# Two sigmoids in place of one in a GRU step, and another order of the first loads

## The chip, the cores and the metric

One core of one Trainium2 chip runs the kernel, as one program. The time is device microseconds (us) of that core for one execution. Smaller is better. The kernel before takes 594.6 us, the median of seven runs from 593.49 to 597.3 us.

## The reference

The input x has 2 sequences of 1024 steps of 256 numbers, all in float32. The first layer adds to x what a two-layer GRU makes of it, and the second adds to that a mixture of experts (a shared one, and two of eight experts for each token). Of the GRU, all that matters here is one step. Its gates r (reset), z (update) and n (new) are made of a product of the step's input and a product of the state before it:

```python
h0 = zeros; mixed = tanh(x @ W_in.T + b_in + context)
xg = mixed @ Wih.T + bih                 # all steps at once
def step(h, xt):                         # 1024 times, one after the other
    hg = h @ Whh.T + bhh
    r = sigmoid(xr + hr)
    z = sigmoid(xz + hz)
    n = tanh(xn + r * hn)
    return (1 - z) * n + z * h
```

The second layer of the GRU runs the same step over the states of the first.

## The kernel before

**The stages.** The kernel loads its weights, runs both GRU layers, and then the mixture of experts (`moe`). The change lies in the GRU and in the loads ahead of it. At the very end stands a second, slow GRU behind `tc.If`, for inputs on which the first one isn't exact; it isn't taken here.

**The GRU in ticks.** Each sequence of 1024 steps is cut into J = 16 chunks of S = 64 steps that run side by side, and each chunk warms its state up on the steps ahead of it (`AHEAD`: 64 steps for layer 0, 44 for layer 1). So the loop has 64 + 64 + 2 = 130 ticks. Layer 0 runs in ticks 0 to 127, layer 1 in ticks 22 to 129, two steps behind. That makes 128 + 108 = 236 steps of a layer. Two batches times 16 chunks are 32 rows (R); the 256 hidden units lie in four quarters (Q) of 64, each on 32 partitions, so that a gate of all rows is a tile of 128 partitions by 64.

**One step of a layer.** `add_state` (L247) adds the state's product to a PSUM bank in which the input's product already stands. `finish_scanned` then makes the new state:

- L287, ScalarE: one sigmoid over the sums of r and z, 128 by 128, into `gates`. The weights and biases of z were negated at the start, so that this gives 1 - z at once.
- L290, VectorE: a scan, s = r * hn + xn, in the PSUM bank.
- L300, ScalarE: n = tanh, negated.
- L302, VectorE: the part of the state that is kept.
- L305, VectorE: a scan that gives the new state's rows.
- L313, VectorE: the transpose to `h`, which the next tick's L247 needs.

ScalarE also copies the next step's starting sums into a bank (`prepare`, L421): of layer 0 from `inputs`, of layer 1 the bias `bt`. In ticks with both layers, TensorE adds the input's product of layer 1 (`feed`, L219).

**Order.** `tc.manual_schedule` fixes the order of the loop as the code has it. On each engine the instructions run in that order, and wait for each other by semaphores.

**Inputs of layer 0.** `inputs` holds the starting sums of 64 steps. A `mix` piece (L196 products, L208 tanh) makes `mixed` of 256 columns of x (MB); an input piece (L219 products, L366 the bias) makes one step's inputs of it. Two mix pieces and four input pieces stand ahead of the loop; the ticks take the rest, two to a tick while layer 0 runs alone, else one. L354 writes the first quarter of every step's `inputs` (a bias) in one VectorE copy.

**The loads.** SP's queue issues, in this order: `w_in`, the first 512 columns of x (two loads), `wih0`, `whh0`, `wih1`, `whh1`, the rest of x, and the weights of `moe`. ScalarE's queue issues `vec`, and eight loads that spread the biases over the partitions (`both`, L126). L165 to L169 add the biases up (`bt`).

Of the kernel before, what the change touches and what calls it, by code (L numbers as in the profile page):

```python
# [8 lines left out]
FP = mybir.dt.float32  # L9
# [3 lines left out]
AF = mybir.ActivationFunctionType  # L13
ALU = mybir.AluOpType
# [3 lines left out]
P = 128  # L18
# [3 lines left out]
KD = D // P  # L22
N = B * T
# [3 lines left out]
Q = 4  # L27
U = D // Q
WIDE = 6 * U + 8
R = P // Q  # L30
J = R // B
S = T // J
# [9 lines left out]
TB = 512  # L42
MB = 256
# [20 lines left out]
def gru_moe(ctx, tc, xT, vec, bias, w_in, wih0, whh0, wih1, whh1, w_out, w_gate, router, w1, w3, w2, w1e, w2e, out):  # L64
    nc = tc.nc
    const = ctx.enter_context(tc.tile_pool(name="const", bufs=1))

    def weights(src, k, m, name, pool=const):
        t = pool.tile([P, k, m], FP, name=name)
        nc.sync.dma_start(out=t, in_=src.rearrange("(k p) m -> p k m", p=P))  # L70
        return t
# [5 lines left out]
    def cols(i):  # L77
        return slice(R * i, R * (i + 1))
# [5 lines left out]
    x_sb = const.tile([P, KD, N], FP, name="x_sb")  # L84
    xT_v = xT.rearrange("(k p) n -> p k n", p=P)

    def load_x(n0):
        for k in range(KD):
            nc.sync.dma_start(out=x_sb[:, k, n0 : n0 + TB], in_=xT_v[:, k, n0 : n0 + TB])

    load_x(0)
    hs1 = const.tile([P, KD, N], FP, name="h1")
    count = const.tile([P, 1], I32, name="count")
    ones = const.tile([P, 1], FP, name="ones")
# [15 lines left out]
    class Steps:  # L110


        def __init__(self, stack, tag, on_pe, less_z):
            def pool(name, **kw):
                return stack.enter_context(tc.tile_pool(name=name + tag, **kw))

            self.gru_only = gru_only = pool("gru_only", bufs=1)
            self.edge = edge = pool("edge", bufs=1)
            self.step_pool = pool("step", bufs=3)
            self.p_step, self.p_mix = pool("p_step", bufs=1, space=PSUM), pool("p_mix", bufs=2, space=PSUM)  # L120
            self.sums, self.rows, self.states, self.starts, self.start_rows = ({} for _ in range(5))
            both = []
            for layer in range(2):
                t = edge.tile([P, 2, 3, U], FP, name=f"both{layer}")
                for q in range(Q):
                    nc.scalar.dma_start(  # L126
                        out=t[cols(q)].rearrange("p i g u -> p (i g u)"),
                        in_=bias[layer, q : q + 1, :].to_broadcast([R, 2 * 3 * U]),
                    )
                both.append(t)  # L130
            wih0_sb = weights(wih0, KD, 3 * D, "wih0_sb", gru_only)
            whh0_sb = weights(whh0, KD, 3 * D, "whh0_sb", gru_only)
            wih1_sb = weights(wih1, KD, 3 * D, "wih1_sb", gru_only)
            whh1_sb = weights(whh1, KD, 3 * D, "whh1_sb", gru_only)
            self.wih, self.whh = (wih0_sb, wih1_sb), (whh0_sb, whh1_sb)
            if less_z:

                for t, i, engine in (
                    (wih0_sb, 1, nc.vector),
                    (whh0_sb, 2, nc.vector),  # L140
                    (wih1_sb, 1, nc.gpsimd),
                    (whh1_sb, 2, nc.gpsimd),
                ):
                    part = t.rearrange("p k (q g u) -> p (k q) g u", q=Q, g=3)[:, :, i, :]
                    engine.tensor_scalar(part, part, -1.0, None, ALU.mult)  # L145

            self.picks = gru_only.tile([P, Q, R], BF, name="picks")
            nc.gpsimd.memset(self.picks, 0.0)  # L150
            for q in range(Q):
                nc.gpsimd.memset(self.picks[32 * q : 32 * q + 3, q, :], 1.0)
            upto = gru_only.tile([P, 3], FP, name="upto")
            nc.vector.memset(upto, 0.0)
            for q in range(Q):
                for i in range(3):
                    nc.vector.memset(upto[32 * q : 32 * q + i + 1, i : i + 1], 1.0)
            only = gru_only.tile([P, 3], FP, name="only")
            nc.vector.tensor_copy(only, upto)
            nc.vector.tensor_tensor(only[:, 1:3], upto[:, 1:3], upto[:, 0:2], ALU.subtract)  # L160
            self.parts, self.sum_bias = {}, []
            for layer in range(2):
                bt = gru_only.tile([P, 4, U], FP, name=f"bt{layer}")
                self.sum_bias.append(bt)
                nc.vector.tensor_copy(bt[:, 0, :], both[layer][:, 1, 2, :])  # L165
                nc.vector.tensor_tensor(bt[:, 1:3, :], both[layer][:, 0, 0:2, :], both[layer][:, 1, 0:2, :], ALU.add)
                nc.vector.tensor_copy(bt[:, 3, :], both[layer][:, 0, 2, :])
                if less_z:
                    nc.vector.tensor_scalar(bt[:, 2, :], bt[:, 2, :], -1.0, None, ALU.mult)  # L169
                if layer not in on_pe:  # L170
                    continue
                part = gru_only.tile([P, 4, U], BF, name=f"part{layer}")
                for i in range(3):
                    rounded = edge.tile([P, 4, U], BF, name=f"rounded{layer}{i}")
                    nc.vector.tensor_copy(rounded, bt)
                    if i < 2:
                        rest = edge.tile([P, 4, U], FP, name=f"rest{layer}{i}")
                        nc.vector.tensor_tensor(rest, bt, rounded, ALU.subtract)
                        bt = rest
                    if i == 0:  # L180
                        nc.vector.tensor_scalar(part, rounded, only[:, 0:1], None, ALU.mult)
                    else:
                        nc.vector.scalar_tensor_tensor(part, rounded, only[:, i : i + 1], part, ALU.mult, ALU.add)
                self.parts[layer] = part
            self.mixed_pool = pool("mixed", bufs=2)
# [92 lines left out]
        def finish_scanned(self, layer, to, tick, after_n, between):  # L278

            ps, h = self.sums[layer], self.rows[layer]
            sums = by_sum(ps)

            gates = self.gates[layer][tick % 2]
            nc.scalar.activation(gates[:, :, :, 1], sums[:, 1:3, :], AF.Sigmoid)  # L287

            s = ps[:, 4 : 4 + 6 * U : 3]
            nc.vector.tensor_tensor_scan(  # L290
                s,
                gates[:, 0, :, :].rearrange("p u i -> p (u i)"),
                ps[:, 0 : 6 * U : 3],
                0.0,
                ALU.mult,
                ALU.add,
            )

            n = self.step_pool.tile([P, U, 2], FP, name=f"n{layer}")
            nc.scalar.activation(n[:, :, 0], s[:, 1 : 2 * U : 2], AF.Tanh, scale=-1.0)  # L300
            after_n()
            nc.vector.scalar_tensor_tensor(n[:, :, 1], gates[:, 1, :, 1], 1.0, h, ALU.subtract, ALU.mult)  # L302
            between()
            row = self.step_pool.tile([P, U, 2], FP, name=f"row{layer}")
            nc.vector.tensor_tensor_scan(  # L305
                row.rearrange("p u i -> p (u i)"),
                gates[:, 1, :, :].rearrange("p u i -> p (u i)"),
                n.rearrange("p u i -> p (u i)"),
                0.0,
                ALU.mult,  # L310
                ALU.subtract,
            )
            nc.vector.transpose(to, row[:, :, 1])  # L313
            self.rows[layer], self.states[layer] = row[:, :, 1], to
# [16 lines left out]


    with ExitStack() as stack:
        g = Steps(stack, "", on_pe=(), less_z=True)
        g.gates = [
            [g.gru_only.tile([P, 2, U, 2], FP, name=f"gates{layer}{i}") for i in range(2)] for layer in range(2)
        ]
# [1 line left out]
            for t in pair:  # L339
                nc.gpsimd.memset(t, 0.0)  # L340
        for n0 in range(TB, N, TB):
            load_x(n0)
        load_later()
        edge = g.edge
        h0_pool = stack.enter_context(tc.tile_pool(name="h0", bufs=4))
# [5 lines left out]


        inputs = g.gru_only.tile([P, S, 4, U], FP, name="inputs")
        nc.vector.tensor_copy(inputs[:, :, 0, :], g.sum_bias[0][:, 0, :].unsqueeze(1).to_broadcast([P, S, U]))  # L354

        def input_piece(i):

# [17 lines left out]
        for bank in banks[0] + banks[1]:  # L375
            for q in range(Q):
                nc.tensor.matmul(
                    out=bank[cols(q), 0 : 6 * U],
# [76 lines left out]
        mixing, making = mix_pieces(), input_pieces()  # L455

        def take(pieces, n):
            return [p for _, p in zip(range(n), pieces)]
# [13 lines left out]
                    yield from take(which, 1)  # L472
            yield from making

        for piece in take(mixing, 2) + take(making, 4):
            for part in piece:
                part()
        in_turn = pieces_in_turn()
# [52 lines left out]
    with tc.tile_pool(name="p_gate", bufs=1, space=PSUM) as p_gate:  # L531
        ps = p_gate.tile([P, KD, B], FP, name="ps_gate")
        for m in range(KD):
            for k in range(KD):
                nc.tensor.matmul(
                    out=ps[:, m, :],
# [11 lines left out]
    for k in range(KD):  # L548
        for b in range(B):
            i = COND + k * B + b  # L550
# [7 lines left out]
    n_fit = nc.values_load(count[0:1, 0:1], min_val=0, max_val=P)  # L558
    with tc.If(n_fit < P):
        with ExitStack() as stack:  # L560
            g = Steps(stack, "_turn", on_pe=(0, 1), less_z=False)

            for n0 in range(0, N, TB):
                load_x(n0)
            all_mixed = g.gru_only.tile([P, KD, N], FP, name="all_mixed")
            for n0 in range(0, N, MB):
                mixed, pieces = g.mix(n0)
# [485 lines left out]
```

## Time and profile before

| what | value |
|---|---|
| median of seven runs | 594.6 us |
| the profiled execution | 594.44 us, of which the span of the trace is 592.6 us |
| loads and first pieces, to the first gates of tick 0 | 0 to 19.01 us |
| ticks of layer 0 alone (22) | gates at 19.01, then one tick every 2.8 us |
| ticks of both layers (106) | about 80 to 375 us |
| mixture of experts | the rest |
| busy: TensorE, VectorE, ScalarE, GpSimd | 552.2, 399.8, 253.2, 75.9 us |

In a view of the timeline, each line has the start, the duration, the engine, the line of the kernel, the operation, what it writes and reads with shapes, and in brackets how long the engine had been idle and what ended that. An instruction's duration includes its start and its drain, so that instructions on one engine may overlap by a part of it. A `q` behind an engine's name means its sequencer (a DMA being issued, for instance). Ends of matmuls are modelled.

### The profile page before, as it was taken

What the parts mean: (1) busy time and instruction counts of PE and PEld (TensorE: products, weight loads), DVE (VectorE), ACT (ScalarE), POOL (GpSimd) and SP (SyncE); (2) the same over time, 40 slices, a digit from 0 to 9 for tenths busy, and PEclk for the clock granted to TensorE, in tenths of its full rate; (3) what the DMA queues carried; (4) which work ended last, traced back from release to release, by engine and by line L of the source; (5) the groups of instructions that cost most, each with busy time, mean ns of one, the idle gap of its engine ahead of it and who ended that gap; (6) DMA issues with size and microseconds to landing.
All of it is one profiled execution on the core that took longest, in us unless ns stands there. A gap on an engine that the chain in (4) does not pass through costs nothing. (4 is left out here: it accounts for less than half of the span.)

```text
span 592.6 us, 18629 instructions
## 1 busy us (share of the span) xinstructions
PE 552.2 (93%) x7508; PEld 349.5 (59%) x7508; DVE 399.8 (67%) x1300; ACT 253.2 (43%) x849; POOL 75.9 (13%) x115
## 2 busy tenths in 40 slices
PE   4999999999999899999999999589999999999995
PEld 2555566667655444544545455347448888874584
DVE  3556678888988788888888888743884333324485
ACT  1333356666656566656666666301223333331100
POOL 1200000000000000000000000100037760007750
PEclk9999999999999999999999999879999999999999
DMA  8950000000000000000000000002114563113351
GB/s 280 363 187 2 1 3 4 4 2 2 4 2 3 2 3 2 2 3 3 3 2 3 3 3 3 1 19 89 36 32 141 167 152 82 63 64 90 111 167 66
DMA packets 22845, 32.12 MB, mean 54 GB/s; under 512 B 3200, under 2 KB 17920, under 8 KB 22752
## 3 DMA queue, kind: packets, MB, share of 16 engines
q1 hardware_dynamic: 18816, 21.12, 10.5%
q0 software_dynamic: 3408, 9.31, 6.2%
q8 instruction: 63, 1.03, 0.7%
q10 hardware_dynamic: 528, 0.40, 0.3%
q14 instruction: 30, 0.25, 0.1%
HBM read 21.52 MB, written 9.31 MB: 52 GB/s over the span
## 5 line engine op out<-in xcount | busy, mean ns | idle before, releaser
L247 PE MATMUL ps_step<-whh_sb,h 128*32 128x192 f32 x3712 | 197.5, 330 | 2.8 <-DVE h L313 2.8
L247 PEld LDWEIGHTS ps_step<-whh_sb,h 128*32 128x32 f32 x3712 | 97.5, 109 | 77.1 <-DVE h L313 60.2
L219 PE MATMUL ps_step<-wih_sb,h 128*32 128x192 f32 x1728 | 127.0, 331 | 11.0 <-ACT ps_step L421 2.5
L305 DVE TENSOR_TENSOR_SCAN row<-gates,n 128x128 f32<-128x128 f32 x236 | 100.2, 425 | 38.5 <-ACT n L300 38.5
L290 DVE TENSOR_TENSOR_SCAN ps_step<-gates,ps_step 128x128 f32<-128x128 f32 x236 | 98.5, 417 | 25.1 <-ACT gates L287 25.1
L300 ACT ACTIVATE n<-ps_step 128x64 f32<-128x64 f32 x236 | 55.0, 233 | 118.8 <-DVE ps_step L290 118.8
L219 PEld LDWEIGHTS ps_step<-wih_sb,h 128*32 128x32 f32 x1728 | 58.9, 109 | 58.8 <-ACT ps_step L421 45.8
L287 ACT ACTIVATE gates<-ps_step 128x128 f32<-128x128 f32 x236 | 68.7, 291 | 39.0 <-PE ps_step L247 35.7
L219 PE MATMUL ps_in<-wih_sb,mixed 128*32 128x192 f32 x1024 | 59.8, 334 | 6.0 <-DVE wih_sb L145 3.4
L313 DVE STREAM_TRANSPOSE h<-row 128x64 f32<-128x64 f32 x236 | 58.0, 246 | 8.1
L902 DVE COPY hT<-ps_hT 128x256 f32<-128x256 f32 x39 | 16.6, 425 | 54.4 <-PE ps_hT L900 54.4
L421 ACT COPY ps_step<-inputs 128x256 f32<-128x256 f32 x128 | 49.7, 388 | 4.9 <-DVE inputs L366 4.9
L219 PEld LDWEIGHTS ps_in<-wih_sb,mixed 128*32 128x32 f32 x1024 | 35.6, 112 | 23.2 <-ACT ps_step L421 6.7
L302 DVE SCALAR_TENSOR_TENSOR n<-gates,row 128x64 f32<-128x64 f32 x232 | 48.4, 209 | 0.0
L640 POOL IOTA lane_i<- 128x128 int32 x1 | 0.2, 240 | 363.9 <-DVE row L305 363.9
L937 POOL DMA_INDIRECT xg<-given,pick x39 | 37.2, 953 | 65.6 <-DVE more L891 54.0
L421 ACT COPY ps_step<-bt 128x256 f32<-128x256 f32 x108 | 40.7, 377 | 3.4
L908 PE MATMUL ps_y<-w2e_sb,hT 128*128 x156 | 40.2, 380 | 1.0 <-DVE hT L902 1.0
L908 PE MATMUL ps_h<-w1e_sb,xT 128*128 x156 | 40.2, 380 | 0.7 <-DVE xT L902 0.7
L978 POOL DMA_INDIRECT yb<-back,slots x32 | 30.7, 960 | 56.3 <-DMA back<-y 46.8
L908 PEld LDWEIGHTS ps_y<-w2e_sb,hT 128*128 128x128 f32 x156 | 29.4, 190 | 5.5 <-DVE hT L902 1.5
L948 ACT ACTIVATE he<-ps_h 128x256 f32<-128x256 f32 x39 | 15.0, 384 | 37.6 <-PE ps_h L908 37.6
(165 smaller groups left out, 492.2 us busy)
## 6 DMA issues: line engine op xcount, KB each, us to landing
back<-y SPq DMA_DIRECT2D x39, 128.0 KB, 1.8
x_sb<-in_xT SPq DMA_DIRECT2D x8, 256.0 KB, 6.1
w1e_sb<-in_w1e SPq DMA_DIRECT2D x1, 2048.0 KB
w2e_sb<-in_w2e SPq DMA_DIRECT2D x1, 2048.0 KB, 18.5
given<-base SPq DMA_DIRECT2D x4, 512.0 KB, 2.8
out_dram<-o SPq DMA_DIRECT2D x16, 128.0 KB, 2.1
wih_sb<-in_wih SPq DMA_DIRECT2D x2, 768.0 KB, 7.7
whh_sb<-in_whh SPq DMA_DIRECT2D x2, 768.0 KB, 7.8
```

The lines of the kernel that those rows point to most:

```text
L219: last = nc.tensor.matmul(out=out[cols(q), :, :], lhsT=given(k), rhs=self.wih[layer][:, k, q * 3 * U : (q + 1) * 3 * U].rearrange("p (g u) ...
L247: nc.tensor.matmul(out=by_sum(self.sums[layer])[cols(q), 0:3, :], lhsT=self.states[layer][:, k, :], rhs=self.whh[layer][:, k, q * 3 * U : ...
L287: nc.scalar.activation(gates[:, :, :, 1], sums[:, 1:3, :], AF.Sigmoid)
L290: nc.vector.tensor_tensor_scan(s, gates[:, 0, :, :].rearrange("p u i -> p (u i)"), ps[:, 0 : 6 * U : 3], 0.0, ALU.mult, ALU.add,)
L300: nc.scalar.activation(n[:, :, 0], s[:, 1 : 2 * U : 2], AF.Tanh, scale=-1.0)
L302: nc.vector.scalar_tensor_tensor(n[:, :, 1], gates[:, 1, :, 1], 1.0, h, ALU.subtract, ALU.mult)
L305: nc.vector.tensor_tensor_scan(row.rearrange("p u i -> p (u i)"), gates[:, 1, :, :].rearrange("p u i -> p (u i)"), n.rearrange("p u i -> p ...
L313: nc.vector.transpose(to, row[:, :, 1])
L421: return nc.scalar.copy(by_sum(banks[layer][tick % 2])[:, 0:4, :], g.sum_bias[1] if layer else inputs[:, position(0, tick) % S, :, :],)
L908: nc.tensor.matmul(out=ps, lhsT=of[:, k, :], rhs=weights_sb[:, bass.ds(e * KD + k, 1), :], start=(k == 0), stop=(k == KD - 1),)
L937: nc.gpsimd.indirect_dma_start(out=xg, out_offset=None, in_=given[:, :], in_offset=bass.IndirectOffsetOnAxis(ap=pick[:, i : i + 1], axis=0),)
L978: nc.gpsimd.indirect_dma_start(out=yb, out_offset=None, in_=back[:, :], in_offset=bass.IndirectOffsetOnAxis(ap=slots[:, c, j : j + 1], axi ...
```

## The change

- The sigmoid of a step becomes two of 128 by 64: one for r, and one of the negated sum of z (scale -1.0), which gives 1 - z. The negations of four weights (L145) and of two biases (L169) go.
- The biases are laid out for all 128 partitions by the host, and come in one load on SP's queue, behind the first x.
- The first load of x has 256 columns in place of 512; the other 256 stand behind `wih0` and `whh0`.
- Each load of x is one DMA for both halves (k).
- The copy L354 covers 8 steps on VectorE, and the other 56 on GpSimd.
- Two input pieces stand ahead of the loop, not four; the ticks take the other two.

```diff
-    def load_x(n0):
-        for k in range(KD):
-            nc.sync.dma_start(out=x_sb[:, k, n0 : n0 + TB], in_=xT_v[:, k, n0 : n0 + TB])
-    load_x(0)
+    def load_x(n0, n):
+        nc.sync.dma_start(out=x_sb[:, :, n0 : n0 + n], in_=xT_v[:, :, n0 : n0 + n])
+    load_x(0, MB)
...
-            both = []
-            for layer in range(2):
-                t = edge.tile([P, 2, 3, U], FP, name=f"both{layer}")
-                for q in range(Q):
-                    nc.scalar.dma_start(
-                        out=t[cols(q)].rearrange("p i g u -> p (i g u)"),
-                        in_=bias[layer, q : q + 1, :].to_broadcast([R, 2 * 3 * U]),
-                    )
-                both.append(t)
+            both = edge.tile([P, 2, 2, 3, U], FP, name="both")
+            nc.sync.dma_start(out=both.rearrange("p l i g u -> p (l i g u)"), in_=bias)
             wih0_sb = weights(wih0, KD, 3 * D, "wih0_sb", gru_only)
             whh0_sb = weights(whh0, KD, 3 * D, "whh0_sb", gru_only)
+            rest_of_x()
             wih1_sb = weights(wih1, KD, 3 * D, "wih1_sb", gru_only)
             whh1_sb = weights(whh1, KD, 3 * D, "whh1_sb", gru_only)
...
-            if less_z:
-                for t, i, engine in (
-                    (wih0_sb, 1, nc.vector),
-                    (whh0_sb, 2, nc.vector),
-                    (wih1_sb, 1, nc.gpsimd),
-                    (whh1_sb, 2, nc.gpsimd),
-                ):
-                    part = t.rearrange("p k (q g u) -> p (k q) g u", q=Q, g=3)[:, :, i, :]
-                    engine.tensor_scalar(part, part, -1.0, None, ALU.mult)
...
-                if less_z:
-                    nc.vector.tensor_scalar(bt[:, 2, :], bt[:, 2, :], -1.0, None, ALU.mult)
...
-            nc.scalar.activation(gates[:, :, :, 1], sums[:, 1:3, :], AF.Sigmoid)
+            nc.scalar.activation(gates[:, 0, :, 1], sums[:, 1, :], AF.Sigmoid)
+            nc.scalar.activation(gates[:, 1, :, 1], sums[:, 2, :], AF.Sigmoid, scale=-1.0)
...
-        g = Steps(stack, "", on_pe=(), less_z=True)
+        g = Steps(stack, "", on_pe=(), rest_of_x=lambda: load_x(MB, TB - MB))
...
-        nc.vector.tensor_copy(inputs[:, :, 0, :], g.sum_bias[0][:, 0, :].unsqueeze(1).to_broadcast([P, S, U]))
+        for engine, i, n in ((nc.vector, 0, MB // R), (nc.gpsimd, MB // R, S - MB // R)):
+            engine.tensor_copy(
+                inputs[:, i : i + n, 0, :], g.sum_bias[0][:, 0, :].unsqueeze(1).to_broadcast([P, n, U])
+            )
...
-        for piece in take(mixing, 2) + take(making, 4):
+        for piece in take(mixing, 2) + take(making, 2):
...
-        "bias": bias,
+        "bias": np.repeat(bias.reshape(Q, -1), R, axis=0),
```

More of the change, by code (lines that the diff above doesn't have):

```diff
@@ L110, in gru_moe, with __init__ @@
     class Steps:
[L113 removed]
+        def __init__(self, stack, tag, on_pe, rest_of_x):
             def pool(name, **kw):
@@ L164, in __init__ @@
                 self.sum_bias.append(bt)
-                nc.vector.tensor_copy(bt[:, 0, :], both[layer][:, 1, 2, :])
-                nc.vector.tensor_tensor(bt[:, 1:3, :], both[layer][:, 0, 0:2, :], both[layer][:, 1, 0:2, :], ALU.add)
-                nc.vector.tensor_copy(bt[:, 3, :], both[layer][:, 0, 2, :])
-                if less_z:
-                    nc.vector.tensor_scalar(bt[:, 2, :], bt[:, 2, :], -1.0, None, ALU.mult)
+                nc.vector.tensor_copy(bt[:, 0, :], both[:, layer, 1, 2, :])
+                nc.vector.tensor_tensor(bt[:, 1:3, :], both[:, layer, 0, 0:2, :], both[:, layer, 1, 0:2, :], ALU.add)
+                nc.vector.tensor_copy(bt[:, 3, :], both[:, layer, 0, 2, :])
                 if layer not in on_pe:
@@ L341, in gru_moe @@
         for n0 in range(TB, N, TB):
-            load_x(n0)
+            load_x(n0, TB)
         load_later()
@@ L560, in gru_moe @@
         with ExitStack() as stack:
-            g = Steps(stack, "_turn", on_pe=(0, 1), less_z=False)
-            for n0 in range(0, N, TB):
-                load_x(n0)
+            g = Steps(stack, "_turn", on_pe=(0, 1), rest_of_x=lambda: load_x(0, N))
             all_mixed = g.gru_only.tile([P, KD, N], FP, name="all_mixed")
@@ L1021 @@
     bias = np.stack(
-        [np.concatenate([quarters(a[f"L0_cond_b{n}{i}"]).reshape(Q, 3 * U) for n in ("ih", "hh")], 1) for i in range(2)]
+        [quarters(a[f"L0_cond_b{n}{i}"]).reshape(Q, 3 * U) for i in range(2) for n in ("ih", "hh")], axis=1
     )
```

## The prediction

> **What bounds the kernel now.** I read the busy times first, then the counts of the costliest groups, then the timeline: of a tick with layer 0 alone, of a tick with both layers, and of the first 20 us. TensorE is busy 93% of the span, but that doesn't make it the bound of the loop; the timeline does.
>
> A tick of layer 0 alone, from one gate sigmoid to the next:
>
> ```profile
> 52.56 0.30 ACT L287 ACTIVATE gates<-ps_step 128x128 f32<-128x128 f32 x1 [0.95 <-PE ps_step L247]
> 52.89 0.43 DVE L290 TENSOR_TENSOR_SCAN ps_step<-gates,ps_step 128x128 f32<-128x128 f32 x1 [0.86 <-ACT gates L287]
> ...
> 53.35 0.23 ACT L300 ACTIVATE n<-ps_step 128x64 f32<-128x64 f32 x1 [0.49 <-DVE ps_step L290]
> 53.47 0.39 ACT L421 COPY ps_step<-inputs 128x256 f32<-128x256 f32 x1
> 53.61 0.42 DVE L305 TENSOR_TENSOR_SCAN row<-gates,n 128x128 f32<-128x128 f32 x1 [0.18 <-ACT n L300]
> ...
> 54.07 0.25 DVE L313 STREAM_TRANSPOSE h<-row 128x64 f32<-128x64 f32 x1
> ...
> 54.37 0.48 PEld L247 LDWEIGHTS ps_step<-whh_sb,h 128*32 128x32 f32 x16 [0.33 <-DVE h L313]
> ...
> 55.36 0.30 ACT L287 ACTIVATE gates<-ps_step 128x128 f32<-128x128 f32 x1 [1.50 <-PE ps_step L247]
> ```
>
> Each starts when the one above it ends (L421 aside): 0.33 + 0.46 + 0.26 + 0.46 + 0.30 + 0.99 = 2.80 us. This is a chain of latencies, and the sigmoid is a link of it. In a tick with both layers:
>
> ```profile
> 355.03 0.43 DVE L290 TENSOR_TENSOR_SCAN ps_step<-gates,ps_step 128x128 f32<-128x128 f32 x1
> ...
> 356.02 0.29 ACT L287 ACTIVATE gates<-ps_step 128x128 f32<-128x128 f32 x1
> 356.22 0.25 DVE L313 STREAM_TRANSPOSE h<-row 128x64 f32<-128x64 f32 x1
> 356.39 0.40 DVE L290 TENSOR_TENSOR_SCAN ps_step<-gates,ps_step 128x128 f32<-128x128 f32 x1
> 356.52 0.48 PEld L247 LDWEIGHTS ps_step<-whh_sb,h 128*32 128x32 f32 x16 [0.33 <-DVE h L313]
> ...
> 357.44 0.29 ACT L287 ACTIVATE gates<-ps_step 128x128 f32<-128x128 f32 x1
> ...
> 357.77 0.43 DVE L290 TENSOR_TENSOR_SCAN ps_step<-gates,ps_step 128x128 f32<-128x128 f32 x1
> ```
>
> Layer 0's scans are 355.03 and 357.77, layer 1's is 356.39. From 355.03 the same chain takes 2.74 us to the next scan of layer 0, so it binds here too, and layer 1 fits in between. VectorE has little room: layer 1's scan starts 0.17 us behind layer 0's transpose, and 0.08 us after its own gates' end (356.31).
>
> The opening:
>
> ```profile
> 6.21 3.75 PE L196 MATMUL ps_mix<-x_sb,w_in_sb 128*128 128x256 f32 x8 [2.85 <-DMA x_sb<-in_xT]
> 10.25 0.20 DVE L165 COPY bt<-both 128x64 f32<-128x64 f32 x1 [6.02 <-DMA both<-in_bias]
> 10.45 1.14 ACT L208 ACTIVATE mixed<-ps_mix,mix_bias 128x128 f32<-128x128 f32 x4 [7.68 <-DVE bt L165]
> 10.67 2.29 DVE L354 COPY inputs<-bt 128x4096 f32<-128x4096 f32 x1
> 12.87 0.42 DVE L145 TENSOR_SCALAR wih_sb<-wih_sb 128x512 f32<-128x512 f32 x1
> 13.39 2.70 PE L219 MATMUL ps_in<-wih_sb,mixed 128*32 128x192 f32 x32 [3.43 <-DVE wih_sb L145]
> 15.21 0.54 DVE L165 COPY bt<-both 128x64 f32<-128x64 f32 x1 [1.49 <-DMA both<-in_bias]
> 16.09 0.61 DVE L366 TENSOR_TENSOR inputs<-ps_in,bt 128x192 f32<-128x192 f32 x2
> 19.01 0.29 ACT L287 ACTIVATE gates<-ps_step 128x128 f32<-128x128 f32 x1 [2.15 <-PE ps_step L247]
> ```
>
> The biases are late twice (10.25 and 15.21), the copy L354 and the negation L145 hold VectorE until TensorE may start at 13.39, and L366 stands behind the second bias. Nothing of this hides anything: the first gates are at 19.01.
>
> **The ticks.** One might expect the scan to start earlier, as it needs r alone, and n's row (128x64, same stride, 0.233 us) prices r's sigmoid below the 0.291 us of the row of both gates. But in the program as built, r's sigmoid raises no semaphore. Its count is added by z's sigmoid, right behind it, and the scan waits for that sum. So both sigmoids are on the chain. Two in a row never occur in the trace before; the nearest row is n followed by a copy that waits for nothing: 53.35 to 53.47, so 0.12 us from start to start. So z starts 0.12 behind r and ends at 0.12 + 0.233 = 0.353 us, against 0.291: 0.062 us more. From below, z could follow r by its elements alone, 0.291 - 0.233 = 0.058, and end at 0.291: nothing more. From above, it could wait for r's end: 0.466, or 0.175 more. I take 0.062, as the row of n and its copy is this engine with this shape in this place.
>
> The Trainium skill ("ScalarE: Activation LUTs", section "What ACT_TABLE_LOAD costs") gives an ACTIVATE a fixed 186 ns and 0.833 ns per element, with an overlap of about 93 ns back to back; its 293 and 239 ns agree with the rows, its overlap is below the row's 0.11 us, and by it the pair would cost 0.092 us more, 12.0 us over 130 ticks.
>
> The path around layer 1 moves alike: its gates reach its scan 0.06 later, from which n, the copy of `bt` and layer 0's next gates follow on ScalarE; between 86 and 89 us that path has no slack either (copy 86.05, gates 86.36), but a tick holds layer 1's delay there once and VectorE's 1.37 us once, so it too gives 2.74 + 0.06. I also see a separate wait for TensorE ahead of each scan on VectorE; the products end before the gates start, so I cost it at nothing. Behind that wait stand L302 and L305 of the layer, for which the next product waits. If it cost VectorE 0.03 us where its scan follows the transpose, the ticks would take 3 us more.
>
> 130 ticks by 0.062 are **8.1 us more**; the bounds are 0 and 22.8 us.
>
> **The opening.** Added up from the rows: `w_in` and the first x are 512 KB as before (`w_in` and the first half of x), so TensorE starts its mixing at about 6.2 again and ends at about 9.7 (3.75 us less a wait of 0.26 for the second half). The biases stand third on the queue, at about 7 to 8; ScalarE has no bias loads to issue, so the tanh of the second piece runs when the products end, to about 10.4. `wih0` was issued at 2.29 and took 7.7 us, so landed at 10.0; before it there were 1.5 MB of SP's loads and part of the 0.4 MB of biases, now 1.7 MB: I keep 10.0. `whh0` landed at 12.3 (6.09 and 6.2), and is now issued some 3 us earlier, past the biases but ahead of the rest of x: 11.5 to 12.3. Two input pieces take 2.70 us cold or 1.70 warm, from 10.4 at the latest: 12.1 to 13.1, L366 and L421 of the first one beside the second. The state's product and the gates take 1.0 us more (18.03 to 19.01): gates at 13.1 to 14.1, so 4.9 to 5.9 us earlier. I take **5.2 us less**.
>
> The rest of x and layer 1's weights are needed later: the former by tick 0's mix piece, behind the product, at 13 to 14 (2.7 MB into the queue; 0.7 us of slack ahead of tick 1's product if it is late), the latter from tick 21 on. The two input pieces that move into the loop stretch its ticks with pieces by two; such a tick takes 86.36 to 89.10 = 2.74 us, the same as one without (357.44 to 360.18), so they cost nothing; uncovered, they would cost TensorE's 0.83 us each. The negations of L145 on GpSimd and VectorE are gone with their 3.9 us, already in the sum.
>
> GpSimd's copy has 56 by 64 = 3584 elements. Nearest rows: the cast of 128 elements at 0.287 and of 8 at 0.188 us give 0.83 ns each, so 3.1 us; L145 on GpSimd, 512 elements in 1.546 us, gives 10.8 us. It starts with the finished biases at about 8.5 and is needed by tick 7's L421. Either is in time, unless it holds up VectorE. The nearest row is L165 at 15.21 under GpSimd's L145 (15.09 to 16.64): 0.54 instead of 0.20 us, held up by 0.34 and not to the end. So I cost it at 0 to 0.3 us. The Trainium skill ("SBUF — State Buffer", its rule of the shared port pair) says that a VectorE copy of this kind or one with two SBUF inputs blocks fully until GpSimd's instruction ends; by that and 3.1 us nothing is lost, as 11.6 is before the first L366.
>
> **Sum.** The profiled execution took 594.44 us (592.6 of span, 1.8 around it), 0.16 below the median. 594.44 + 8.1 - 5.2 = **597.3 us**, slower by 0.5%. About 0.3%, 1.8 us, is what a measurement of this kernel can tell from no change.
>
> **Rivals.**
> 1. Opening and ticks cancel (within 592.8 to 596.4): a tick cost of 0.03 to 0.05, or 6 us and more gained. For it: the terms are close, and 5.2 / 130 = 0.040 us per tick is break-even. Chance 0.24.
> 2. Faster: ScalarE streams z right behind r, so that a tick costs under 0.027 us more and at the least nothing: 594.44 - 5.2 = 589.2. Against it: the 0.12 of n and its copy. In the same direction lies a scan that is released by r alone: 0.058 by 130 = 7.5 less, so 581.7; the waits as built exclude it. Chance 0.08.
> 3. The pair costs 0.09 us or more, or VectorE's extra wait shows: 130 by 0.09 = 11.7, less 5.2, gives 600.9; with no overlap at all 612.0. Chance 0.13.
> 4. GpSimd's copy takes 10.8 us and blocks VectorE: its first L366 waits to about 19.3, the first gates come at about 20.5, and the opening loses 1.5 us: 604.0. Against it: the 0.34 us above. Chance 0.06.
>
> My forecast, 596.4 to 600, has the rest, 0.49. That makes slower 0.49 + 0.13 + 0.06 = 0.68, same 0.24, faster 0.08. The range goes from 594.0 (tick cost 0.042 with 5.9 gained) to 602.0 (0.097 with 5.0 gained), which leaves out some 0.1 at each end.
>
> **What would show it.** Right: the two sigmoids start 0.12 us apart, the scan starts 0.39 us after r (0.33 before), ticks take 2.86 us with one layer and 2.80 with two, and the first gates are at 13 to 14 us. Wrong: ticks of 2.74 (rival 2), of 2.83 and more (rival 3), VectorE's copy ending with GpSimd's (rival 4), or first gates before 12.5 us.

## The result, and the profile after

The changed kernel takes 596.3 us, the median of 17 runs, against 594.8 us for 44 runs of the kernel before beside it: a ratio of 1.0026, with a 95% interval of 1.0016 to 1.0035. It is slower by about 1.5 us. The table sets the two profiled executions side by side; the times in the loop are starts of r's sigmoid (or, before, of the one sigmoid).

| what | before | after |
|---|---|---|
| the profiled execution, and its span | 594.44, 592.6 us | 596.25, 594.5 us |
| first gates | 19.01 us | 13.35 us |
| tick of layer 0 alone, of both layers | 2.80, 2.74 us | 2.85, 2.79 us |
| last gates, in tick 129 | 380.72 us | 382.72 us |
| from the first gates to the last | 361.71 us | 369.37 us |
| busy: ScalarE | 253.2 us | 264.0 us |

So the opening gives back 5.66 us, the loop takes 7.66 us, and the 2.0 us between them pass through the mixture of experts (1.9 us in the span). In the kernel after, L228 is the state's product, L272 and L287 are the two scans, L282 is the tanh, L295 the transpose, L406 ScalarE's copy and L351 the addition of the bias to an input piece.

The timeline of a tick with layer 0 alone, after:

```profile
53.72 0.23 ACT L268 ACTIVATE gates<-ps_step 128x64 f32<-128x64 f32 x1 [1.50 <-PE ps_step L228]
53.84 0.23 ACT L269 ACTIVATE gates<-ps_step 128x64 f32<-128x64 f32 x1
54.10 0.43 DVE L272 TENSOR_TENSOR_SCAN ps_step<-gates,ps_step 128x128 f32<-128x128 f32 x1 [0.92 <-ACT gates L269]
...
54.57 0.23 ACT L282 ACTIVATE n<-ps_step 128x64 f32<-128x64 f32 x1 [0.49 <-DVE ps_step L272]
...
56.57 0.23 ACT L268 ACTIVATE gates<-ps_step 128x64 f32<-128x64 f32 x1 [1.50 <-PE ps_step L228]
```

L268 is r, L269 is z. The bracket of the scan names L269: it waits for z, which it doesn't read. z starts 0.12 us behind r, and the scan starts 0.38 us behind r; before, it started 0.33 us behind the one sigmoid (52.56 to 52.89). All later steps keep their distances (0.47 to n, then 0.26 to the second scan, 0.46 to the transpose, 0.30 to the product and 0.98 to the next r). A tick with both layers, after:

```profile
353.43 0.23 ACT L268 ACTIVATE gates<-ps_step 128x64 f32<-128x64 f32 x1
...
353.81 0.43 DVE L272 TENSOR_TENSOR_SCAN ps_step<-gates,ps_step 128x128 f32<-128x128 f32 x1
...
355.00 0.25 DVE L295 STREAM_TRANSPOSE h<-row 128x64 f32<-128x64 f32 x1
355.17 0.40 DVE L272 TENSOR_TENSOR_SCAN ps_step<-gates,ps_step 128x128 f32<-128x128 f32 x1
...
356.22 0.23 ACT L268 ACTIVATE gates<-ps_step 128x64 f32<-128x64 f32 x1
...
356.60 0.43 DVE L272 TENSOR_TENSOR_SCAN ps_step<-gates,ps_step 128x128 f32<-128x128 f32 x1
```

The same 0.38 us, and 2.79 us from tick to tick; the scan at 355.17 is layer 1's. And the opening, after:

```profile
4.68 3.75 PE L177 MATMUL ps_mix<-x_sb,w_in_sb 128*128 128x256 f32 x8 [1.32 <-DMA x_sb<-in_xT]
...
7.40 0.20 DVE L148 COPY bt<-both 128x64 f32<-128x64 f32 x1 [3.49 <-DMA both<-in_bias]
...
7.66 3.17 POOL L337 COPY inputs<-bt 128x3584 f32<-128x3584 f32 x1 [4.17 <-DVE bt L148]
7.71 3.17 DVE L150 COPY bt<-both 128x64 f32<-128x64 f32 x1
...
9.54 1.51 PE L200 MATMUL ps_in<-wih_sb,mixed 128*32 128x192 f32 x32 [1.10 <-DMA wih_sb<-in_wih]
...
11.54 0.61 DVE L351 TENSOR_TENSOR inputs<-ps_in,bt 128x192 f32<-128x192 f32 x2
...
13.35 0.23 ACT L268 ACTIVATE gates<-ps_step 128x64 f32<-128x64 f32 x1 [1.06 <-PE ps_step L228]
```

The biases are there at 7.40 (before at 10.25 and 15.21). But L150, a VectorE copy of 128 by 64 that takes 0.19 us elsewhere, takes 3.17 us here, as long as GpSimd's copy L337 that began 0.05 us ahead of it. TensorE's input pieces start at 9.54, and L351, which adds the bias to them, stands at 11.54 behind what VectorE had left to do.

### The profile page after: what moved, and what is told of

It reads as the page before. It is cut to its first block, busy times and chain, and to the rows that moved or that the text cites. A ratio compares the mean times of both kernels' runs of the same rounds, so it can differ in the third digit from the quotient of the medians.

```text
span 594.5 us, 19082 instructions
## 1 busy us (share of the span) xinstructions
PE 556.6 (94%) x7508; PEld 348.8 (59%) x7508; DVE 400.8 (67%) x1296; ACT 264.0 (44%) x1085; POOL 76.0 (13%) x114
## 5 line engine op out<-in xcount | busy, mean ns | idle before, releaser
L228 PE MATMUL ps_step<-whh_sb,h 128*32 128x192 f32 x3712 | 197.5, 330 | 3.4 <-DVE h L295 3.4
L228 PEld LDWEIGHTS ps_step<-whh_sb,h 128*32 128x32 f32 x3712 | 97.7, 109 | 78.7 <-DVE h L295 61.9
L200 PE MATMUL ps_step<-wih_sb,h 128*32 128x192 f32 x1728 | 130.9, 331 | 10.4 <-ACT ps_step L406 1.1
L287 DVE TENSOR_TENSOR_SCAN row<-gates,n 128x128 f32<-128x128 f32 x236 | 100.2, 425 | 38.4 <-ACT n L282 37.4
L272 DVE TENSOR_TENSOR_SCAN ps_step<-gates,ps_step 128x128 f32<-128x128 f32 x236 | 98.2, 416 | 31.3 <-ACT gates L269 28.1
L282 ACT ACTIVATE n<-ps_step 128x64 f32<-128x64 f32 x236 | 54.9, 233 | 118.8 <-DVE ps_step L272 118.8
L268 ACT ACTIVATE gates<-ps_step 128x64 f32<-128x64 f32 x236 | 54.5, 231 | 34.9 <-PE ps_step L228 34.7
L295 DVE STREAM_TRANSPOSE h<-row 128x64 f32<-128x64 f32 x236 | 57.9, 245 | 8.1
L269 ACT ACTIVATE gates<-ps_step 128x64 f32<-128x64 f32 x236 | 53.3, 226 | 0.0
L406 ACT COPY ps_step<-inputs 128x256 f32<-128x256 f32 x128 | 49.6, 388 | 2.8 <-DVE inputs L351 2.8
L284 DVE SCALAR_TENSOR_TENSOR n<-gates,row 128x64 f32<-128x64 f32 x232 | 48.5, 209 | 0.0
L406 ACT COPY ps_step<-bt 128x256 f32<-128x256 f32 x108 | 40.7, 377 | 3.4
## 6 DMA issues: line engine op xcount, KB each, us to landing
whh_sb<-in_whh SPq DMA_DIRECT2D x2, 768.0 KB, 11.6
```

The source lines that it names most:

```text
L200: last = nc.tensor.matmul(out=out[cols(q), :, :], lhsT=given(k), rhs=self.wih[layer][:, k, q * 3 * U : (q + 1) * 3 * U].rearrange("p (g u) ...
L228: nc.tensor.matmul(out=by_sum(self.sums[layer])[cols(q), 0:3, :], lhsT=self.states[layer][:, k, :], rhs=self.whh[layer][:, k, q * 3 * U : ...
L268: nc.scalar.activation(gates[:, 0, :, 1], sums[:, 1, :], AF.Sigmoid)
L269: nc.scalar.activation(gates[:, 1, :, 1], sums[:, 2, :], AF.Sigmoid, scale=-1.0)
L272: nc.vector.tensor_tensor_scan(s, gates[:, 0, :, :].rearrange("p u i -> p (u i)"), ps[:, 0 : 6 * U : 3], 0.0, ALU.mult, ALU.add,)
L287: nc.vector.tensor_tensor_scan(row.rearrange("p u i -> p (u i)"), gates[:, 1, :, :].rearrange("p u i -> p (u i)"), n.rearrange("p u i -> p ...
```

## The experiments

The first eight of the nine runs were made on a chip on which the kernel before takes some 653 us. The ticks take the same there as above; what is longer is the mixture of experts. There the engines stand idle for long stretches: in experiment 1 TensorE is busy for 15.4 of the 50 us from 450 to 500, where the profile of the changed kernel above has all 50, and its granted clock is 0.62 in that stretch. What they wait for was not followed, so the longer time isn't shown to come from the lower clock. Line numbers shift with each edit. Ratios are to the kernel before on the same chip: 652.8 us for the runs of the first four experiments, 653.1 us for the next four.

**1. The changed kernel again**, as the base for the others: no edit.

> The changed kernel as it is, beside the others on one chip. Theory: its ticks are 2.85 us with layer 0 alone and 2.79 with both (0.055 more than before, 7 us over 130 ticks), its first gates come 5.7 us earlier; 1.5 to 2 us slower than before. Rival (the opening and the ticks swing from execution to execution): another sign or more than 4 us.

Measured: 654.3 us, ratio 1.0022 (1.0006 to 1.0039). First gates at 12.61, last at 382.06, ticks 2.85 and 2.79, L150 blocked for 3.17 us from 6.97. The result repeats. The opening itself varies from run to run by some tenths, with the landing of the loads (biases at 6.66 here, 7.40 above): in both the first gates stand 5.95 us behind the biases, and likewise in experiment 5 (6.29 and 12.24).

**2. The two sigmoids alone**, in the kernel before.

```diff
-            nc.scalar.activation(gates[:, :, :, 1], sums[:, 1:3, :], AF.Sigmoid)
+            nc.scalar.activation(gates[:, 0, :, 1], sums[:, 1, :], AF.Sigmoid)
+            nc.scalar.activation(gates[:, 1, :, 1], sums[:, 2, :], AF.Sigmoid)
```

> The kernel before, with two sigmoids in place of one and nothing else. Theory (both sigmoids lie on each tick's chain): first gates at 19.0 as before, ticks 2.85 and 2.79, so 130 by 0.055 = 7.2 us slower, near 602. Rival A (the ticks of the changed kernel are longer because of its moved pieces or its other order of loads, not the sigmoids): ticks 2.80 and 2.74, no change. Rival B (the scan needs r alone): ticks of 2.74 and 2.68, 7.5 us faster.

Measured: 660.6 us, ratio 1.0107 (1.0083 to 1.0132), so about 7.0 us more (7.8 by the medians). Ticks take 2.85 and 2.79 us; from the first gates (20.48) to the last (389.77) it is 369.29 us, 7.58 more than before. The split alone brings the longer ticks of the changed kernel. The first gates were expected at 19.0; they came at 20.48, as the second pair of input pieces took 2.79 us (1.70 before) and the state's product 1.51 us (0.82), both of them work that the edit doesn't touch. The first tick, of 3.21 us, has such slow products too (a mix piece of 1.85 us, 1.13 before).

**3. The loads alone**: the changed kernel with one sigmoid, the negations back, and the whole first copy of `inputs` on VectorE.

```diff
+            if less_z:
...
+                    engine.tensor_scalar(part, part, -1.0, None, ALU.mult)
...
-            nc.scalar.activation(gates[:, 0, :, 1], sums[:, 1, :], AF.Sigmoid)
-            nc.scalar.activation(gates[:, 1, :, 1], sums[:, 2, :], AF.Sigmoid, scale=-1.0)
+            nc.scalar.activation(gates[:, :, :, 1], sums[:, 1:3, :], AF.Sigmoid)
...
-        for engine, i, n in ((nc.vector, 0, MB // R), (nc.gpsimd, MB // R, S - MB // R)):
...
+        nc.vector.tensor_copy(inputs[:, :, 0, :], g.sum_bias[0][:, 0, :].unsqueeze(1).to_broadcast([P, S, U]))
```

> The changed kernel with one sigmoid over r and z, the negations of before (weights and biases), and the whole first copy of inputs on VectorE. Theory (the opening's gain stands by itself): ticks 2.80 and 2.74 as before, first gates at 13.5 to 14.5 as a negation of 0.42 us now stands ahead of the first input piece, 4.5 to 5.5 us faster than before, near 590. Rival (earlier loads only move a wait: ticks stall on later loads): first ticks over 3 us and 593 to 595.

Measured: 647.6 us, ratio 0.9912 (0.9888 to 0.9935), so about 5.7 us less (5.2 by the medians). This beats both kernels. First gates are at 12.98, last at 375.07, ticks 2.80 and 2.74. Experiments 2 and 3 take the change apart, though not quite in two: experiment 3 also keeps the negations and has no copy on GpSimd. By the ratios they are +7.0 and -5.7 us, together 1.3 us, against the 1.4 us (0.0022 by 652.8) of experiment 1; by the medians +7.8 and -5.2, together 2.6, against 1.6. Each has an interval of some 1.6 us to either side, so this shows no more than that the parts add up within about 2 us. The negations, which the split was to save, are in this timeline:

```profile
9.72 0.42 DVE L137 TENSOR_SCALAR wih_sb<-wih_sb 128x512 f32<-128x512 f32 x1
...
10.21 1.16 PEld L211 LDWEIGHTS ps_in<-wih_sb,mixed 128*32 128x32 f32 x32 [2.55 <-issue]
...
11.43 0.42 DVE L137 TENSOR_SCALAR whh_sb<-whh_sb 128x512 f32<-128x512 f32 x1
```

TensorE starts its input pieces 0.49 us behind the first negation, and the second stands among the last steps ahead of the first gates. Without negations and with the same copy on VectorE (experiment 4) the first gates come at 11.99, so the negations cost about 1.0 us, once (from one profile of each). The split that saves them costs 0.055 us in each of 130 ticks.

**4. The whole first copy of `inputs` on VectorE**, in the changed kernel.

```diff
-        for engine, i, n in ((nc.vector, 0, MB // R), (nc.gpsimd, MB // R, S - MB // R)):
-            engine.tensor_copy(
-                inputs[:, i : i + n, 0, :], g.sum_bias[0][:, 0, :].unsqueeze(1).to_broadcast([P, n, U])
-            )
+        nc.vector.tensor_copy(inputs[:, :, 0, :], g.sum_bias[0][:, 0, :].unsqueeze(1).to_broadcast([P, S, U]))
```

> The changed kernel with the whole first copy of inputs (64 steps) on VectorE, none on GpSimd. Theory (GpSimd's copy held VectorE's copy of a bias from 7.71 to 10.88 and so the first L351): the bias copies end by 8.5, the big copy by 10.8, the first L351 starts within 0.3 us of its product, first gates at 12.2 to 12.7, 0.7 to 1.1 us faster than the changed kernel. Rival (VectorE's 3.17 us wait was hidden, as the first state's weights land no earlier than 12.3): first gates at 13.3 again.

Measured: 653.7 us, ratio 1.0004 (0.9987 to 1.002). Against experiment 1 that is 0.7 us less by the medians; the first gates are 0.62 us earlier (11.99) and the last 0.57 us (381.49). Its timeline:

```profile
6.79 0.19 DVE L150 COPY bt<-both 128x64 f32<-128x64 f32 x1
...
7.30 2.29 DVE L336 COPY inputs<-bt 128x4096 f32<-128x4096 f32 x1
...
10.16 0.36 DVE L348 TENSOR_TENSOR inputs<-ps_in,bt 128x192 f32<-128x192 f32 x1 [0.58 <-PE ps_in L200]
```

L150 is back at 0.19 us. The copy of all 64 steps on VectorE takes 2.29 us, less than the 3.17 us that GpSimd takes for 56 of them and that VectorE loses beside it. The first addition of the bias (L348) now waits for TensorE; in the changed kernel it is VectorE that is late. The intervals of the two ratios overlap, so the 0.6 us rest on one trace of each kernel. The biases landed at 6.48 here; at the 5.95 us of experiment 1 behind them the changed kernel's first gates would stand at 12.43, so by this estimate 0.4 us are the copy's.

**5. z behind the scan**: z's sigmoid is issued after the scan, so that r alone can release it.

```diff
-            nc.scalar.activation(gates[:, 1, :, 1], sums[:, 2, :], AF.Sigmoid, scale=-1.0)
...
+            nc.scalar.activation(gates[:, 1, :, 1], sums[:, 2, :], AF.Sigmoid, scale=-1.0)
```

> The changed kernel with z's sigmoid written behind the scan, so that r's sigmoid alone releases the scan; as both read one PSUM bank, z's sigmoid now waits for the scan. Theory (the scan of the changed kernel starts late only because the two reads of one bank are put in order, z's first): the scan starts 0.27 us behind r (0.38 in the changed kernel, 0.33 before), z starts 0.46 behind the scan's start and n 0.12 behind z, so the 0.11 gained ahead of the scan is lost ahead of n: ticks of 2.84 to 2.87 and 2.78 to 2.81, the changed kernel's time within 2 us. Rival (what costs the 0.055 is something else, VectorE's extra wait for TensorE for instance, which falls away here): ticks of 2.80 and 2.74 or less, 7 us faster than the changed kernel.

Measured: 714.2 us, ratio 1.0932 (1.0908 to 1.0956); ticks of 3.06 us with layer 0 alone and mostly 3.30 with both. Both the theory and its rival missed. Its timeline:

```profile
52.09 0.23 ACT L268 ACTIVATE gates<-ps_step 128x64 f32<-128x64 f32 x1 [1.71 <-PE ps_step L228]
52.35 0.43 DVE L271 TENSOR_TENSOR_SCAN ps_step<-gates,ps_step 128x128 f32<-128x128 f32 x1 [0.80 <-ACT gates L268]
52.82 0.23 ACT L279 ACTIVATE gates<-ps_step 128x64 f32<-128x64 f32 x1 [0.50 <-DVE ps_step L271]
...
53.08 0.23 DVE L284 SCALAR_TENSOR_TENSOR n<-gates,row 128x64 f32<-128x64 f32 x1 [0.30 <-ACT gates L279]
53.41 0.42 DVE L287 TENSOR_TENSOR_SCAN row<-gates,n 128x128 f32<-128x128 f32 x1
```

The scan does start 0.26 us behind r, 0.12 sooner than in the changed kernel. But now z waits for the scan, of which it reads nothing: it stands 0.47 us behind it, where n stood. L284 needs z, and so joins the chain: 0.26 from z to L284 and 0.33 from L284 to the second scan L287. From the first scan to the second it is now 1.06 us, where it was 0.73. So 0.12 is won and 0.33 lost. My expectation had left out L284, which until then had lain beside n.

That is 0.21 us in a tick of layer 0 alone; with both layers a tick loses 0.51 us, and these ticks make up most of the 60 us. There the two layers follow each other on VectorE, scan behind scan:

```profile
401.11 0.40 DVE L271 TENSOR_TENSOR_SCAN ps_step<-gates,ps_step 128x128 f32<-128x128 f32 x1
...
402.76 0.40 DVE L271 TENSOR_TENSOR_SCAN ps_step<-gates,ps_step 128x128 f32<-128x128 f32 x1
...
404.42 0.40 DVE L271 TENSOR_TENSOR_SCAN ps_step<-gates,ps_step 128x128 f32<-128x128 f32 x1
```

From each layer's first scan to the other's it is 1.65 us and 1.66 us; in the changed kernel it is 1.36 and 1.43 (353.81, 355.17, 356.60). So both layers' longer steps add up in one tick.

This shows who is ordered against whom: in the one order the scan waits for z's sigmoid, in the other z's sigmoid waits for the scan, and neither reads what the other writes. The order is a wait in the program, on a semaphore of the other engine. What they share is `gates`, in different parts, and the PSUM tile `ps_step`, where z's sums lie beside what the scan reads and writes. In the program as built, z keeps its wait for the scan also where r and z get tiles of their own and the scan's result goes to SBUF, so that the PSUM tile is all that they share; that was not run. The Trainium skill ("PSUM — Partial Sum Buffer", section "PSUM bank collisions raise a hardware error") says that two engines may not access one bank and the same 32 partitions at a time, reads included, and that instructions on such a pair of engines are ordered for it, ScalarE against VectorE too. The two traces agree with that (0.26 us from z to the scan, 0.47 from the scan to z). By it, as long as z's sums lie in the bank of r's, the scan can start on r alone only where z's sigmoid waits for the scan. A kernel with them in another bank was not run, since it needs more products.

**6. The biases by eight loads on ScalarE's queue**, in the changed kernel.

```diff
-            both = edge.tile([P, 2, 2, 3, U], FP, name="both")
-            nc.sync.dma_start(out=both.rearrange("p l i g u -> p (l i g u)"), in_=bias)
+            for layer in range(2):
+                t = edge.tile([P, 2, 3, U], FP, name=f"both{layer}")
+                for q in range(Q):
+                    nc.scalar.dma_start(
...
```

> The changed kernel with the biases loaded as before: eight loads on ScalarE's queue. Theory (the biases were the last to come in the opening, 10.25 and 15.2 us): the second layer's bias lands at 14 to 15.5 and stands ahead of the first L351 on VectorE, first gates at 16 to 18, 3 to 5 us slower than the changed kernel. Rival (the weights bind, wih0 at 9.5 and whh0 near 12): first gates within 0.7 us of the changed kernel's.

Measured: 660.1 us, ratio 1.0112 (1.0085 to 1.014). First gates at 18.45, 5.84 us later than in experiment 1; last at 387.83, 5.77 later. In the timeline the two layers' biases are the waits that are left:

```profile
9.81 0.20 DVE L155 COPY bt<-both 128x64 f32<-128x64 f32 x1 [5.61 <-DMA both<-in_bias]
...
15.56 0.20 DVE L155 COPY bt<-both 128x64 f32<-128x64 f32 x1 [1.94 <-DMA both<-in_bias]
```

L358, the addition ahead of the first gates, follows the second at 15.98. The single load of the biases carries the opening's gain: without it the other changes ahead of the loop leave 18.45 us, against 19.01 before. Whether it is the number of the loads, their queue or their place in it was not taken apart. The gates came 0.45 us later than the 18 us that I had put as the upper end; the state's product took 1.51 us here, for 0.86 in experiment 1.

**7. Four input pieces ahead of the loop**, in the changed kernel.

```diff
-        for piece in take(mixing, 2) + take(making, 2):
+        for piece in take(mixing, 2) + take(making, 4):
```

> The changed kernel with four input pieces ahead of the loop, as before. Theory (two pieces moved into the ticks cost nothing there, TensorE having room): ticks 2.85 and 2.79 as in the changed kernel, first gates 0.5 to 1.3 us later (two pieces take 1.5 us, in part beside VectorE's late copies), so 0.5 to 1.3 us slower. Rival (a piece in a tick costs TensorE's 0.83): 0.4 to 1.2 us faster than the changed kernel.

Measured: 654.7 us, ratio 1.0025 (1.0006 to 1.0045). First gates at 13.51 (0.90 later), last at 382.62 (0.56 later), ticks of 2.85 and 2.79. By the last gates, moving the two pieces into the loop brings about half a microsecond, and they are nearly free there. Nearly: with two pieces ahead the fourth tick takes 3.20 us (22.02 to 25.22 after, 21.29 to 24.51 in experiment 1, and likewise in experiments 4 and 9), and with four there is no such tick. In the changed kernel's trace it is this scan that comes late:

```profile
22.86 0.23 ACT L282 ACTIVATE n<-ps_step 128x64 f32<-128x64 f32 x1 [0.50 <-DVE ps_step L272]
22.98 0.39 ACT L406 COPY ps_step<-inputs 128x256 f32<-128x256 f32 x1
...
23.48 0.42 DVE L287 TENSOR_TENSOR_SCAN row<-gates,n 128x128 f32<-128x128 f32 x1 [0.54 <-ACT ps_step L406]
```

It starts 0.62 us behind n, in other ticks 0.26, and the profile puts that down to the copy L406, of which it reads nothing. Experiments 3, 5, 6 and 8 have two pieces ahead and no such tick (3 and 8 with one sigmoid, 5 and 6 with two), so the pieces alone aren't its cause. It stays open.

**8. One sigmoid and no negation**: z enters in its plain form, z * h - (z - 1) * n, by three VectorE instructions in place of L284 and the second scan. The first copy of `inputs` is on VectorE.

```diff
-            nc.vector.scalar_tensor_tensor(n[:, :, 1], gates[:, 1, :, 1], 1.0, h, ALU.subtract, ALU.mult)
+            nc.vector.tensor_tensor(zh, z, h, ALU.mult)
...
-            nc.vector.tensor_tensor_scan(
...
+            nc.vector.scalar_tensor_tensor(zn, z, 1.0, n, ALU.subtract, ALU.mult)
+            nc.vector.tensor_tensor(row, zh, zn, ALU.subtract)
```

> A candidate: the changed kernel's loads, the big copy on VectorE, one sigmoid over r and z without any negation; the new state is made as z*h - (z - 1)*n by three VectorE operations of 128 by 64 (z*h ahead of n) in place of the multiply and the second scan. Theory (the chain is what sets the time): from n to the transpose two short operations of about 0.23 us each stand in place of a scan of 0.46, so ticks of 2.74 to 2.82 and 2.70 to 2.78, first gates at 12 us, 6 to 9 us faster than before. Rival (VectorE has no room, and each dependent operation pays its drain): ticks 0.05 to 0.1 longer, 0 to 6 us slower than that.

Measured: 653.5 us, ratio 1.0009 (0.9992 to 1.0027). First gates at 11.88, ticks 2.85 and 2.79 to 2.80. The rival holds: two short dependent instructions cost more than one scan that is twice as long. Its timeline:

```profile
52.80 0.23 DVE L287 SCALAR_TENSOR_TENSOR zn<-gates,n 128x64 f32<-128x64 f32 x1 [0.17 <-ACT n L282]
53.06 0.22 DVE L288 TENSOR_TENSOR row<-zh,zn 128x64 f32<-128x64 f32 x1
...
53.32 0.24 DVE L289 STREAM_TRANSPOSE h<-row 128x64 f32<-128x64 f32 x1
```

0.26 and 0.26 from start to start are 0.52 us, against 0.46 from the second scan to the transpose: about 0.06 us a tick, by chance close to the price of the split.

**9. All 512 columns of x first**, in the changed kernel, with nothing of x behind the weights. This ran on a chip on which the kernel before took 594.4 us.

```diff
-    load_x(0, MB)
+    load_x(0, TB)
...
-        g = Steps(stack, "", on_pe=(), rest_of_x=lambda: load_x(MB, TB - MB))
+        g = Steps(stack, "", on_pe=(), rest_of_x=lambda: None)
```

> The changed kernel with all 512 columns of x in the first load and nothing behind the weights. Theory: this part of the change is worth little. The other 256 columns are 256 KB ahead of the biases and wih0 on SP's queue; at the rate at which the changed kernel's opening moves its loads that is 0.6 to 0.8 us, so the biases and wih0 land that much later, and TensorE's mixing, which waits for the whole first load, starts at about 5.4 instead of 4.6 to 4.7. The first gates come 0.5 to 0.9 us later than in the changed kernel (12.6 to 13.4 us there), ticks stay at 2.85 and 2.79: about +0.7 us in all, a ratio of 0.0015 above the changed kernel's 1.0022 to 1.0025. Rival: the rest of x behind the weights costs the changed kernel something in its first ticks (one of 3.20 and two of 2.92 us instead of 2.85); without it those ticks fall back to 2.85 and the time is the same or up to 0.3 us less than the changed kernel's.

Measured: 595.9 us, ratio 1.0028 (1.0014 to 1.0041), where the changed kernel has 1.0026. First gates at 13.07, 0.28 us earlier than in the changed kernel's trace. Its timeline:

```profile
6.15 3.75 PE L177 MATMUL ps_mix<-x_sb,w_in_sb 128*128 128x256 f32 x8 [2.78 <-DMA x_sb<-in_xT]
7.09 0.20 DVE L148 COPY bt<-both 128x64 f32<-128x64 f32 x1 [3.21 <-DMA both<-in_bias]
...
7.40 3.17 DVE L150 COPY bt<-both 128x64 f32<-128x64 f32 x1
...
11.25 0.36 DVE L351 TENSOR_TENSOR inputs<-ps_in,bt 128x192 f32<-128x192 f32 x1
```

TensorE's mixing starts 1.47 us later (6.15 for 4.68), and nothing comes of it: VectorE, blocked from 7.40 to 10.57, still ends last, and it goes by the biases' landing, which is 0.31 us earlier in this run (the first gates stand 5.98 us behind it). So the smaller first block of x is worth nothing in the changed kernel that these runs could tell (the intervals of both ratios reach 0.6 to 0.8 us to either side). I had expected 0.5 to 0.9 us, because I looked at the loads and not at what waits last. The rival's time fits, but not its reason: the first ticks are still 2.93, 2.90, 2.85 and 3.20 us.

## Why the prediction was right

**The sum.** The median is 596.3 us, 1.0 below the 597.3 of the forecast and inside its range (594.0 to 602.0), but just below the 596.4 at which the forecast's own band began: by its time alone it could as well be the case of rival 1. What tells them apart is the terms, and neither of that rival's is there (a tick cost of 0.03 to 0.05, or 6 us and more gained). The profiled execution took 1.8 us more than the one before, where 2.9 were forecast. Both terms came out some 0.45 us towards the faster side, which is much in a difference of two terms of 5 to 8 us; that they were not further off is in part luck, as told below.

**The ticks: mechanism right, size a little high.** z's sigmoid is on the chain, started 0.12 us behind r as the row of n and its copy had it, and the scan waits for it; the trace and experiment 2 show it, and experiment 5 that the scan starts sooner where it doesn't wait. The term was 0.062 us a tick and measured 0.055: z's row is 0.226 us where I took n's 0.233. 0.12 + 0.226 - 0.291 gives 0.055. Ticks of 2.85 and 2.79 were forecast at 2.86 and 2.80, and the loop's 7.66 us at 8.1. Of the 7.66, 129 intervals of 0.055 are 7.1 us; the tick of 3.20 us is 0.35 more, which I hadn't forecast, and the two first ticks (2.92 and 2.91, before 2.81 and 2.79) are 0.1 more. So the term itself was 1.0 us too high, and by luck ticks that I didn't foresee made up for half of it.

By the overlap of 93 ns that the Trainium skill ("ScalarE: Activation LUTs", section "What ACT_TABLE_LOAD costs") states, the pair would have cost 0.092 us. The trace has 0.055, and decides against it.

**The extra wait for TensorE: nothing, as costed.** Layer 1's scan still starts 0.17 us behind layer 0's transpose (355.00 to 355.17 after), as before.

**The opening: 5.66 us instead of 5.2, with some steps off.** TensorE's mixing started at 4.68, not at about 6.2: with 256 columns it doesn't wait as it did, although the bytes ahead of it are as many; with all 512 in one load it starts at 6.15. `wih0` landed at 9.54 (10.0 in the working). The two input pieces ran at the warm price of 1.51 us, while the range had 1.70 to 2.70. So each of these steps ran 0.2 to 1.5 us ahead of the working, and the input pieces ended at 11.05, not at 12.1 to 13.1. But the state's product began only at 12.34, behind the additions on VectorE. Most of the lead was lost again in the step that failed, and that the two nearly cancel is luck:

**GpSimd's copy: the duration was right (3.17 for 3.1 us), the hold-up wrong.** I costed it at 0 to 0.3 us, from L165's 0.34 us under GpSimd's negation, and set that row against the rule of the Trainium skill ("SBUF — State Buffer", section "SBUF: two separate sides"), by which the later of two such instructions, here VectorE's copy, blocks until the other ends. In this trace the rule holds: L150 takes 3.17 us, here and in all five experiments that keep GpSimd's copy (1, 5, 6, 7 and 9), and ends 0.05 us behind GpSimd. That VectorE's copy ends with GpSimd's was one of the prediction's signs of being wrong, so that sign was there. My second cover, that 11.6 us is ahead of the first addition of the bias, did not stand either, since TensorE was ready sooner than I thought. Experiment 4 puts what the copy on GpSimd costs, against the same copy on VectorE, at 0.4 to 0.6 us. It is a small error, as the copy didn't take the 10.8 us of rival 4. In experiment 2 the row that misled me reads otherwise too: L165 there starts at 15.30 and ends at 15.71, 0.05 us behind GpSimd's negation (14.16 to 15.66):

```profile
14.16 1.50 POOL L145 TENSOR_SCALAR wih_sb<-wih_sb 128x512 f32<-128x512 f32 x1 [10.66 <-DMA wih_sb<-in_wih]
...
15.30 0.41 DVE L165 COPY bt<-both 128x64 f32<-128x64 f32 x1 [2.53 <-DMA both<-in_bias]
```

Why the same row of the kernel before ended 0.9 us ahead of GpSimd's is not known.

**The moved pieces: nearly free, as costed**, apart from the tick of 3.20 us, if it is theirs, which is not shown.

**The rivals.** The scan released by r alone exists (experiment 5), but only where z is issued behind it, and then z is late. The cancelling case was close: experiment 4, at a ratio of 1.0004, lies in it. The faster case needed one sigmoid (experiment 3), and its time, about 5.7 us below the kernel before, is the opening's term alone.

## What to carry to other kernels

A step on a chain of latencies that recurs 130 times must be weighed against what it saves once: 0.055 us by 130 was more than all the opening's gain of 5.7 us, and the saving of the negations for which it was paid was 1.0 us. Before an instruction is split so that a consumer may start on its first half, look in the program whether the consumer waits for the second half all the same, as the scan did here, where both halves read the consumer's PSUM tile; then the split only adds. Ahead of a hoped-for gain from an earlier load, ask which engine ends last there: 1.47 us on TensorE's start were worth nothing behind a VectorE that was blocked.

## What the runs showed of the hardware

- A VectorE copy of 128 by 64, 0.19 us by itself, took 3.17 us beside a GpSimd copy of 128 by 3584 that had started 0.05 us before it. So moving work to an idle engine stopped a busy one for longer than the work takes there (2.29 us for 4096 elements).
- A sigmoid on ScalarE and a scan on VectorE that use one PSUM tile were ordered one behind the other by waits in the program, in whichever order the code had them, at 0.26 us from the sigmoid to the scan and 0.47 us from the scan to the sigmoid.
- On VectorE, a dependent instruction of 128 by 64 starts 0.26 us behind the one that it needs, and a scan of 128 by 128 starts 0.33 us behind such an instruction; a scan of 128 by 128 is followed at 0.46 us. On ScalarE, two independent sigmoids of 128 by 64 are 0.12 us apart.
